# Two placements in a selective-scan kernel: where the old sum enters PSUM, and where a rounding term stands among the scans

## The chip, the cores and the metric

The kernel runs on one core of a Trainium2 chip. The metric is the device time of one execution in microseconds. Before the change it is 1489.29 us, the median of 3 runs (1488.71 to 1490.92).

## The reference, cut to what matters

Two layers of a state-space image model on a 64x64 image with 96 channels. Each layer normalises, projects to 192 inner channels, convolves 3x3, runs scans over the 4096 pixels in four orders, normalises, gates and projects back. The change touches only the scans of the second layer. Its core is this, with 192 channels and 16 states for each of the four orders:

```
delta = softplus(delta + delta_bias)
...
def step(h, t):
    u_t, d_t, B_t, C_t = t
    h = h * exp(d_t[..., None] * A[None]) + (d_t * u_t)[..., None] * B_t[:, :, None, :]
    y = einsum('bkdn,bkn->bkd', h, C_t)
    return (h, y)
...
y = out_y[:, 0] + out_y[:, 1, :, ::-1] + out_y[:, 2][:, :, i1] + out_y[:, 3][:, :, i2]
```

For each channel and state, h is a first-order recurrence along the pixels, with a decay exp(dt A) and an input dt u B. Then h is multiplied by C and summed over the 16 states, and the sums of the four orders are added.

## The kernel before, in words

**Tiling.** The second layer's scans are done in 16 groups (`GROUPS`, numbered 0 to 15): four orders, each in four chunks of 1024 pixels. In a group there are 24 units, numbered 0 to 23 here: 3 blocks of channels (T) times 8 pairs of states (m). A tile of a unit is 128x1024: 64 channels times two states on the partitions, 1024 pixels along. Units run in the order m = 0, 1 for T = 0, then T = 1, then T = 2 (units 0 to 5), then m = 2, 3, and so on. So T = 0, 1, 2 start with units 0, 2 and 4, and end with units 19, 21 and 23.

**What a unit does.** PSUM tile `b` first receives the factor B. For an even unit TensorE picks rows of B (`b<-B,selh`, `stage_B`), and VectorE multiplies by du in place, which is called the product here (`b<-b,du`, `stage_b`). For an odd unit ScalarE has already made products in another layout (`bT<-duT,BT`), and TensorE transposes them into PSUM (`b<-ident,bT`, `stage_t`), so VectorE has no product to make. Even units use PSUM tile b0, odd units b1, so each is refilled only after the scan two units before. ScalarE makes the decay (`a<-dt,am`, `stage_a`), VectorE runs the recurrence (`h<-a,b`, with `carry` when a chunk continues another, `stage_s`). GpSimd multiplies by C (`hc<-h,cb`, `stage_c`). TensorE sums over the partitions into the block's PSUM tile with a fold matrix (`ys<-hc,fold`, `stage_r`). After the last pair of states ScalarE copies that tile to y (`y<-ys`, `stage_y`).

**The old sum.** y already holds what earlier orders added. It enters the block's PSUM tile first, as a matmul of y with the identity (`ys<-y,ident`), and the folds of the 8 pairs are accumulated on top. Before the change this matmul stands in `stage_r` of the block's first unit, just ahead of that unit's fold. There is one PSUM tile for each T, so it can be filled only when `stage_y` of the group before has emptied it.

**C rows.** Each pair's C rows come from DRAM into one of 3 SBUF buffers (`cb<-C`, `fetch_c`), issued on SP's queue.

**Preparing the next group.** Beside the units of a group, the next groups' projections and step sizes are made (`prelude`). `pj<-u,xw` are the projections, in two halves, made a group further ahead (two groups before their use). `pd<-xd,dwb` is the argument of the softplus for one T. From it ScalarE makes |pd|, relu(pd), w = exp(-|pd|), ln = log(1 + w), and the rounded 1 + w written back to PSUM (`pd<-w,one`, step `plus`). VectorE then makes what that rounding added, (1 + w) - 1 - w (`w<-pd,w`, 128x512, step `missed`; the rounding term). GpSimd takes it off the logarithm (`ln<-ln,w`, step `found`), adds the relu (`sp<-sp,ln`, `whole`) and multiplies by u (`su<-sp,u`, `times`). The tiles w and ln exist once, so the next T's w waits for `found`, its ln for `whole`. Later SP's queue spreads sp and su to the dt and du tiles (`dt<-sp`, `du<-su`, four transfers each for each T).

**Order.** Every engine runs in program order here: the class `Ordered` wraps each call, and therefore nearly all these instructions carry its line, L859. The order is that of the main loop over j, the running number of units. A pass of the loop is called a slot here, numbered within its group like its unit. In slot j the loop issues, in this order: C transfers; `stage_B` or `stage_t` for unit j+1; a waiting `pd` matmul; the decay of unit j+2; the product, if j is even; `stage_r` of unit j-3 (LAG is 3); the scan of unit j; the carry of j-1; `stage_y` of unit j-4; `stage_c` of unit j-1; then the prelude steps due in that slot. `delta(T)` gives each of its steps a place in `slots`, plus 4T. In groups from 2 on `plus` and the logarithm stand in slots 1, 5 and 9, and `missed` in slots 2, 6 and 10, at the end of the slot, therefore behind that slot's scan. The `pd` matmul for T = 1 and 2 is issued in slots 3 and 7, the first half of `pj` in slot 11.

Of the kernel before, what the change touches and what calls it, by code (L numbers as in the profile page):

```python
# [44 lines left out]
def two_ss2d_layers(  # L45
# [678 lines left out]
    def scans(weights):  # L724

        xw, dwb, _ = weights
        with ExitStack() as sc:  # L730
            pre = sc.enter_context(tc.tile_pool(name="fpre", bufs=1))
            mn = sc.enter_context(tc.tile_pool(name="fmn", bufs=2))
            pps = sc.enter_context(tc.tile_pool(name="fps", bufs=1, space=PSUM))
            dram = sc.enter_context(tc.tile_pool(name="fdram", bufs=2, space=DRAM))
            carry = pre.tile([128, 3, NP], F32, name="fcarry")
            sums = pre.tile([128, 3], F32, name="fsums")
            xd = pre.tile([128, TC], F32, name="fxd")
            nc.vector.memset(xd[96:128], 1.0)
            halves = [slice(0, HT), slice(HT, TC)]
            load_exp_ln()  # L740

            def chunk(k, p, d, c):
                first = c == (NCH - 1 if d else 0)
                cols = TC // HW
                us = []
                for T in range(3):
                    ps = pps.tile([128, TC], F32, tag="m", name=f"fu{k}_{T}")
                    for h in range(2):
                        if p == 0:
                            nc.tensor.matmul(  # L750
                                ps[:, halves[h]], wide[h], u[T][:, HT * c : HT * (c + 1)],
                                start=True, stop=True,
                            )
                            continue
                        for q, s in enumerate(halves):
                            w0 = cols * c + cols // 2 * q
                            nc.tensor.matmul(
                                of_columns(ps[:, s], h), wide[h],
                                columns(u[T], h, slice(w0, w0 + cols // 2)), start=True, stop=True,
                            )  # L760
                    t = pre.tile([128, TC], F32, tag=f"us{T}", name=f"fus{k}_{T}")
                    nc.scalar.copy(t, ps)
                    us.append(t)
                ps = pps.tile([128, TC], F32, tag="m", name=f"fpj{k}")[0:NC]
                for s in halves:
                    for T in range(3):
                        nc.tensor.matmul(
                            ps[:, s], xw[0:64, 0, T, :], us[T][0:64, s],
                            start=(T == 0), stop=(T == 2),
                        )  # L770
                nc.scalar.copy(xd[0:NC], ps)
                C = dram.tile([NS, TC], F32, tag="C", name=f"fC{k}")
                nc.sync.dma_start(out=C, in_=xd[NC - NS : NC])
                B3 = pre.tile([NB, TC], BF16, tag="B3", name=f"fB3{k}")
                left = pre.tile([NB, TC], F32, tag="left", name=f"fleft{k}")
                nc.scalar.copy(B3, xd[0:NB])
                for r, of in ((32, xd), (64, xd), (64, left)):
                    q = slice(r, r + 32)
                    nc.gpsimd.tensor_sub(left[q], of[q], B3[q])
                    nc.gpsimd.tensor_copy(B3[q], left[q])  # L780

                for T in range(3):
                    ps = pps.tile([128, TC], F32, tag="m", name=f"fpd{k}_{T}")
                    for s in halves:
                        nc.tensor.matmul(
                            ps[:, s], dwb[96 : NC + 1, 0, T, :], xd[96 : NC + 1, s],
                            start=True, stop=True,
                        )
                    w, ln, t, dt, du, S = (
                        pre.tile([128, TC], F32, tag=nm, name=f"f{nm}{k}_{T}")  # L790
                        for nm in ("w", "ln", "t", "dt", "du", "S")
                    )
                    nc.scalar.activation(w, ps, AF.Abs)
                    nc.vector.tensor_scalar_max(dt, ps, 0.0)
                    nc.scalar.activation(w, w, AF.Exp, scale=-1.0)
                    nc.scalar.activation(t, w, AF.Identity, bias=one)
                    nc.scalar.activation(ln, w, AF.Ln, bias=one)
                    nc.vector.tensor_scalar_add(t, t, -1.0)
                    nc.vector.tensor_sub(w, w, t)
                    nc.vector.tensor_add(ln, ln, w)  # L800
                    nc.vector.tensor_add(dt, dt, ln)
                    nc.vector.tensor_mul(du, dt, us[T])
                    nc.vector.tensor_tensor_scan(
                        along(d, S), one.to_broadcast([128, TC]), along(d, dt),
                        0.0 if first else sums[:, T : T + 1], ALU.mult, ALU.add,
                    )
                    nc.scalar.copy(sums[:, T : T + 1], along(d, S)[:, TC - 1 : TC])
                    yp = pps.tile([128, TC], F32, tag="y", name=f"fy{k}_{T}")
                    for m in range(NP):
                        cb, a, b, wt, h = (  # L810
                            mn.tile([128, TC], F32, tag=nm, name=f"f{nm}{k}_{T}_{m}")
                            for nm in ("cb", "a", "b", "wt", "h")
                        )
                        row_of(C, m, cb)
                        B = pps.tile([128, TC], F32, tag="B", name=f"fB{k}_{T}_{m}")
                        for s in halves:
                            nc.tensor.matmul(B[:, s], pick(0, m), B3[:, s], start=True, stop=True)
                        nc.scalar.activation(a, dt, AF.Exp, scale=am[:, 0, 0, T, m : m + 1])
                        nc.scalar.activation(
                            wt, S, AF.Tanh, bias=lneps, scale=am[:, 1, 0, T, m : m + 1]  # L820
                        )
                        nc.vector.tensor_mul(b, B, du)
                        nc.vector.scalar_tensor_tensor(b, wt, 1.0, b, ALU.add, ALU.mult)
                        nc.vector.tensor_tensor_scan(
                            along(d, h), along(d, a), along(d, b),
                            0.0 if first else carry[:, T, m : m + 1], ALU.mult, ALU.add,
                        )
                        nc.scalar.copy(carry[:, T, m : m + 1], along(d, h)[:, TC - 1 : TC])
                        nc.gpsimd.tensor_mul(cb, h, cb)
                        for s in halves:  # L830
                            nc.tensor.matmul(
                                yp[:, s], fold2, cb[:, s], start=(m == 0), stop=(m == NP - 1)
                            )
                    for h, half in enumerate(HALF):
                        if p == 0:
                            to, of = y[T][half, HT * c : HT * (c + 1)], yp[half, halves[h]]
                        else:
                            to = columns(y[T][half], h, slice(cols * c, cols * (c + 1)))
                            of = of_columns(yp[half], h)
                        nc.vector.tensor_add(to, of, to)  # L840

            for k, (p, d, c) in enumerate(GROUPS):
                chunk(k, p, d, c)

    def scans(weights):

        xw, dwb, _ = weights  # L850
        class Ordered:
            def __init__(self, engine):
                self.engine = engine

            def __getattr__(self, name):
                op = getattr(self.engine, name)


                return lambda *args, **more: tc.keep_in_program_order(op(*args, **more))  # L859

        pe, act, dve, pool, sp = (
            Ordered(e) for e in (nc.tensor, nc.scalar, nc.vector, nc.gpsimd, nc.sync)
        )
        with ExitStack() as sc:
# [6 lines left out]
            LAG = 3  # L871
            halves = [slice(0, HT), slice(HT, TC)]
            state = [{} for _ in GROUPS]
            early = []

            xd = pre.tile([128, TC], F32, name="xd")
            dve.memset(xd[96:128], 1.0)
# [933 lines left out]
```

## Time and profile before

| what | value |
|---|---|
| median of 3 runs | 1489.29 us (1488.71 to 1490.92) |
| the profiled execution's own time | 1487.71 us |
| its span | 1485.9 us |
| second layer's groups, first scan of group 0 to last scan | about 285 to 1453 us |
| busy: VectorE (DVE), TensorE (PE), ScalarE (ACT), GpSimd (POOL) | 1354.1, 1233.7, 1209.1, 1100.7 us |
| scans of the groups (384) | 2.34 us with a carry, 2.28 us without |
| products (`b<-b,du`) | 1208 ns each |
| rounding terms (`w<-pd,w`) | 45, 665 ns each |
| old-sum matmuls (`ys<-y,ident`) | 120 records, median 592 ns |

The profile is of one execution. Its page gives busy time of each engine, waits and a chain of work; the timeline gives single instructions as start, length, engine, line, operation, output<-inputs and shapes, and in brackets the idle time before it with what ended it. A row can merge several instructions (x2, x6). A table by stretches gives, for each, its length, the busy time of PE, weight loads, DVE, ACT and POOL, TensorE's granted clock (1.00 is full) and the share and rate of the DMA engines. Ends of matmuls are modelled, and a matmul of fp32 data is recorded in several passes.

### The profile page before, as it was taken

How to read it: one execution, taken by the hardware profiler on the slowest of the kernel's cores; microseconds unless marked ns; L12 is line 12 of the kernel's file. 1: busy time of each engine (PE TensorE's matmuls, PEld its weight loads, DVE VectorE, ACT ScalarE, POOL GpSimd, SP SyncE). 2: the span in 40 equal slices, each digit the busy share in tenths (PEclk: the TensorE clock that was granted, in tenths of full speed). 3: DMA queues.
4: the chain of work that ended last, by engine and by line, in shares of the span. 5: the costliest groups of instructions: out<-in, count | busy, mean ns of one | idle time of the engine just before them, and what ended most of it. 6: DMA issues, size and time to landing. Idle time of an engine off the chain costs nothing.

```text
span 1485.9 us, 17265 instructions
## 1 busy us (share of the span) xinstructions
PE 1233.7 (83%) x5091; PEld 488.2 (33%) x5091; DVE 1354.1 (91%) x953; ACT 1209.1 (81%) x2492; POOL 1100.7 (74%) x595
## 2 busy tenths in 40 slices
PE   6954989688888888888887989888888888887887
PEld 3333333323232323333333333333333333322332
DVE  5957778679989999999999999999999999999998
ACT  6564355779889988998999999999998989897872
POOL 1003000479979999989898989898989898989891
PEclk9966988589899999999999999999999999999999
DMA  4230602516252626262626262626262626262534
GB/s 113 73 97 3 160 22 86 129 45 139 60 125 63 143 61 149 64 149 59 151 57 144 57 143 59 142 59 142 59 143 62 145 64 145 67 145 68 134 103 109
DMA packets 79793, 146.30 MB, mean 98 GB/s; under 512 B 27676, under 2 KB 30940, under 8 KB 79596
## 3 DMA queue, kind: packets, MB, share of 16 engines
q1 hardware_dynamic: 78540, 142.78, 39.2%
q0 software_dynamic: 576, 1.57, 0.4%
q8 instruction: 41, 0.67, 0.2%
q10 hardware_dynamic: 576, 0.79, 0.2%
q14 instruction: 60, 0.49, 0.1%
HBM read 80.85 MB, written 12.13 MB: 63 GB/s over the span
## 4 chain that ended last, share of the span: by engine, by line
DVE 30%; issue 21%; PE 14%; ACT 12%; POOL 6%; DMA 5%; SPq 3%; DVEq 0%; ACTq 0%; POOLq 0%
DVE h L859 19%; DVE b L859 8%; ACT a L859 4%; POOL hc L859 4%; PE ys L859 4%; PE pj L859 3%; ACT bT L859 3%; PE b L859 2%; SPq L859 2%; PE cp L1463 2%; DMA szt<-szd 1%; DMA xT<-xs 1%; PE in L1410 1%; PE pd L859 1%; POOL ln L859 1%
## 5 line engine op out<-in xcount | busy, mean ns | idle before, releaser
L859 POOL TENSOR_TENSOR hc<-h,cb 128x1024 f32<-128x1024 f32 x384 | 904.0, 2375 | 97.4 <-DVE h L859 47.1
L859 DVE TENSOR_TENSOR_SCAN h<-a,carry,b 128x1024 f32<-128x1024 f32 x288 | 664.9, 2337 | 27.9 <-PE b L859 5.9
L859 ACT ACTIVATE a<-dt,am 128x1024 f32<-128x1024 f32 x384 | 438.1, 1141 | 65.6 <-DVE h L859 60.5
L859 PE MATMUL ys<-hc,fold 128*64 128x512 f32 x1536 | 431.9, 642 | 1.3 <-POOL hc L859 1.2
L859 ACT ACTIVATE bT<-duT,BT 128x192 f32<-128x192 f32 x1012 | 387.4, 445 | 4.6 <-PE b L859 2.4
L859 PE MATMUL b<-ident,bT 128*128 128x128 f32 x1536 | 222.1, 289 | 25.3 <-DVE h L859 18.6
L859 DVE TENSOR_TENSOR b<-b,du 128x1024 f32<-128x1024 f32 x192 | 231.9, 1208 | 8.3 <-PE b L859 8.3
L859 DVE TENSOR_TENSOR_SCAN h<-a,b 128x1024 f32<-128x1024 f32 x96 | 216.3, 2278 | 12.4 <-POOL hc L859 3.0
L859 PEld LDWEIGHTS b<-ident,bT 128*128 128x128 f32 x1536 | 176.9, 147 | 149.2 <-DVE h L859 90.8
L859 PE MATMUL b<-B,selh 96*128 96x512 bf16 x384 | 117.5, 388 | 128.4 <-DVE h L859 128.0
L859 PEld LDWEIGHTS ys<-hc,fold 128*64 128x64 f32 x1536 | 78.2, 139 | 143.4 <-issue 104.2
L859 PEld LDWEIGHTS <-selh 96*128 96x128 bf16 x384 | 25.7, 98 | 257.6 <-DVE h L859 203.9
L859 PE MATMUL pj<-u,xw 64*124 64x512 f32 x192 | 101.1, 676 | 3.8 <-ACT sz L1445 2.0
L1488 DVE SCALAR_TENSOR_TENSOR acc<-pad,v,acc 128x1052 f32<-128x1052 f32 (+1 forms) x80 | 91.3, 1201 | 0.7
L859 POOL DMA_DIRECT2D du<-su x12 | 6.4, 536 | 82.9 <-ACT am L235 80.6
L261 POOL MEMSET nna<- 128x4 f32 (+1 forms) x9 | 1.0, 117 | 85.9 <-ACT nna L261 85.9
L859 PE MATMUL ys<-y,ident 128*128 128x512 f32 (+1 forms) x120 | 61.4, 616 | 0.0
L859 ACT CAST B<-pj 96x512 bf16<-96x512 f32 (+2 forms) x96 | 54.9, 575 | 6.3 <-PE pj L859 6.3
L859 POOL TENSOR_TENSOR sp<-sp,ln 128x512 f32<-128x512 f32 x45 | 57.9, 1286 | 0.2
L859 POOL TENSOR_TENSOR ln<-ln,w 128x512 f32<-128x512 f32 x45 | 58.0, 1288 | 0.0
L859 POOL TENSOR_TENSOR su<-sp,u 128x512 f32<-128x512 f32 x45 | 57.8, 1285 | 0.0
L859 PE MATMUL pd<-xd,dwb 29*64 29x512 f32 x192 | 57.6, 675 | 0.0
(185 smaller groups left out, 1195.1 us busy)
## 6 DMA issues: line engine op xcount, KB each, us to landing
cb<-C SPq DMA_DIRECT2D x256, 256.0 KB
dt<-sp SPq DMA_DIRECT2D x192, 128.0 KB
du<-su SPq DMA_DIRECT2D x180, 128.0 KB
szd<-sz SPq DMA_DIRECT2D x24, 256.0 KB
szt<-szd SPq DMA_DIRECT2D x24, 256.0 KB
xT<-xs SPq DMA_DIRECT2D x8, 384.0 KB
xs<-xT SPq DMA_DIRECT2D x1, 1536.0 KB
xs<-xT SPq DMA_DIRECT2D x8, 192.0 KB
```

What stands on the lines that cost most here:

```text
L261: return lambda *args, **more: tc.keep_in_program_order(op(*args, **more))
L859: return lambda *args, **more: tc.keep_in_program_order(op(*args, **more))
L1410: nc.tensor.matmul(ps[half], ipw_s[:, 64 * b : 64 * b + 64], xn[:, g * 512 : (g + 1) * 512], start=True, stop=True,)
L1463: nc.tensor.matmul(ps.rearrange("p (r w) -> p r w", w=HW), diag[:, k, :], pad[b][:, c, i : i + SR, j : j + HW], start=(k == 0), stop=(k == ...
L1488: nc.vector.scalar_tensor_tensor(acc, src, wk, acc, ALU.mult, ALU.add)
```

## The change

Three edits. First, a function `scans` is deleted that a later one of the same name replaces. Second, the old-sum matmul moves out of `stage_r` into a new function `start_sum`, which is put into the list of steps for the ends of slots 1, 2 and 4 (T = 0, 1, 2); it stood in slots 3, 5 and 7. The -1 puts it ahead of the other steps of its slot. Third, in groups from 2 on `missed` isn't issued where it stands but kept in a list `between`, and `plus` still stands in slot 1 + 4T; `missed` is now due at the end of that slot as well, and the loop issues it in the next slot behind the product and ahead of `stage_r` and the scan. For group 1 it is issued at once, where it was.

```diff
-    def scans(weights):
...
-            for k, (p, d, c) in enumerate(GROUPS):
-                chunk(k, p, d, c)
...
-            early = []
+            early, between = [], []
...
                     def missed():
 
-                        dve.scalar_tensor_tensor(
-                            me["w", T], me.pop(("pd", T)), -1.0, me["w", T], ALU.add, ALU.subtract
-                        )
+                        def step():
+                            dve.scalar_tensor_tensor(
+                                me["w", T], me.pop(("pd", T)), -1.0, me["w", T],
+                                ALU.add, ALU.subtract,
+                            )
+
+                        between.append(step) if k > 1 else step()
...
-                    o, slots = 4 * T, (-1, -1, -1, 0, 1, 1, 2, 3, 4, 5)
+                    o, slots = 4 * T, (-1, -1, -1, 0, 1, 1, 1, 3, 4, 5)
...
+            def start_sum(k, T):
+                p, d, c = GROUPS[k]
+                ps = live["y", T] = pps.tile([128, HT], F32, tag=f"y{T}", name=f"ys{k}_{T}")
+                parts = [(chunk(y[T], c), lambda s: s)] if (p, d) != (1, 0) else views(y[T], c)
+                for q, (view, f) in enumerate(parts):
+                    pe.matmul(f(ps), ident, view, start=(q == 0), stop=False)
+
             def stage_r(j):
...
-                if m == 0:
-                    ps = live["y", T] = pps.tile([128, HT], F32, tag=f"y{T}", name=f"ys{j}")
-
-                    parts = [(chunk(y[T], c), lambda s: s)] if (p, d) != (1, 0) else views(y[T], c)
-                    for q, (view, f) in enumerate(parts):
-                        pe.matmul(f(ps), ident, view, start=(q == 0), stop=False)
                 ps = live["y", T]
...
+            steps += [
+                (PER * k + (1, 2, 4)[T], -1, partial(start_sum, k, T))
+                for k in range(len(GROUPS)) for T in range(3)
+            ]
...
                 if j % 2 == 0:
                     unit(stage_b, j)
+                while between:
+                    between.pop(0)()
                 unit(stage_r, j - LAG)
                 unit(stage_s, j)
```

More of the change, by code (lines that the diff above doesn't have):

```diff
@@ L729, in scans @@
         xw, dwb, _ = weights
[L730 to L752, printed above, removed]
-                            )
[L754 to L840, printed above, removed]
-            for k, (p, d, c) in enumerate(GROUPS):
-                chunk(k, p, d, c)
@@ L845, in scans @@
-    def scans(weights):
-        xw, dwb, _ = weights
         class Ordered:
@@ L1024, in missed @@
                     def missed():
-                        dve.scalar_tensor_tensor(
-                            me["w", T], me.pop(("pd", T)), -1.0, me["w", T], ALU.add, ALU.subtract
-                        )
+                        def step():
[4 more added lines that the diff above has]
+                        between.append(step) if k > 1 else step()
                     def found():
```

## The prediction

> **What bounds the kernel now.** I read the head of the page, VectorE's waits in the sixteen groups (300 to 1460 us), and timelines of single groups. Below, "unit" is one of the 24 scans of a group, "slot" the loop pass of the same number.
>
> ```profile
> PE 1233.7 (83%) x5091; PEld 488.2 (33%) x5091; DVE 1354.1 (91%) x953; ACT 1209.1 (81%) x2492; POOL 1100.7 (74%) x595
> ```
>
> and the waits (total us, times, longest):
>
> ```profile
> DVE h L859 <- PE b L859: 7.1, 6, 2.5
> DVE b L859 <- PE b L859: 6.6, 6, 4.0
> DVE h L859 <- POOL hc L859: 3.0, 2, 2.6
> ```
>
> VectorE leads, and in the groups it waits for under 20 us in all. The timeline of group 4, units 10 and 11, on VectorE and then on ScalarE (start, length):
>
> ```profile
> 618.90 1.21 DVE L859 TENSOR_TENSOR b<-b,du 128x1024 f32<-128x1024 f32 x1
> 620.24 2.29 DVE L859 TENSOR_TENSOR_SCAN h<-a,b 128x1024 f32<-128x1024 f32 x1
> 622.44 0.67 DVE L859 SCALAR_TENSOR_TENSOR w<-pd,w 128x512 f32<-128x512 f32 x1
> 623.02 2.27 DVE L859 TENSOR_TENSOR_SCAN h<-a,b 128x1024 f32<-128x1024 f32 x1
> ```
>
> ```profile
> 619.65 0.72 ACT L859 ACTIVATE ln<-w,one 128x512 f32<-128x512 f32 x1 [0.75 <-POOL sp L859]
> 620.28 0.67 ACT L859 ACTIVATE pd<-w,one 128x512 f32<-128x512 f32 x1
> ```
>
> The scan starts 0.13 us after the product that it reads has ended; neighbours that don't read each other overlap by 0.08. So a group of VectorE alone is 12 x 5.84 (product, two scans, their joints) + 3 x 0.58 (rounding terms less overlap) = 71.8 us. Measured from scan 0 to scan 0, groups 5 to 14 take 72.24 on average.
>
> A second loop is as long. GpSimd of group 5 and SP's queue behind it:
>
> ```profile
> 669.34 4.68 POOL L859 TENSOR_TENSOR hc<-h,cb 128x1024 f32<-128x1024 f32 x2 [2.95 <-DMA cb<-C]
> ...
> 708.23 11.67 POOL L859 TENSOR_TENSOR hc<-h,cb 128x1024 f32<-128x1024 f32 x5
> ...
> 741.59 4.67 POOL L859 TENSOR_TENSOR hc<-h,cb 128x1024 f32<-128x1024 f32 x2 [1.47 <-DMA cb<-C]
> ```
>
> ```profile
> 717.62 1.08 SPq L859 DMA_DIRECT2D cb<-C  x2
> ...
> 736.08 2.46 SPq L859 DMA_DIRECT2D cb<-C  x4
> ```
>
> From hc of unit 1 to the end of hc of unit 16 (717.60) GpSimd is never idle: 48.3 us, the same within 0.12 in eight groups. That end frees a cb buffer; SP then issues 30 transfers in a row (19 to 20 us), the last being cb of pair 1, which lands about 4 us later and lets the next group's hc 1 begin. hc 1 starts follow each other by 72.18 us on average (669.34 to 1391.18, ten groups), about 72.0 without the pieces in which GpSimd waited for VectorE.
>
> TensorE is third. Its clock is granted in steps:
>
> ```profile
> 400.87:404.28 3.41, 1.91 (x9) 0.55 (x8) 3.41 (x3) 2.55 (x7) 3.41 (x3) 1.00 0.00 0
> 404.28:407.69 3.41, 3.41 (x5) 1.31 (x5) 3.28 (x3) 1.70 (x4) 3.41 (x3) 0.50 0.21 72
> 694.41:697.82 3.41, 1.91 (x9) 0.40 (x7) 3.41 (x3) 2.94 (x9) 3.41 (x3) 1.00 0.00 0
> 1349.77:1353.18 3.41, 1.69 (x8) 0.31 (x6) 3.41 (x2) 1.91 (x5) 3.41 (x2) 1.00 0.54 151
> 1353.18:1356.60 3.42, 3.07 (x12) 1.86 (x12) 3.29 (x3) 2.61 (x7) 3.42 (x3) 0.50 0.56 150
> ```
>
> (stretch and length, TensorE busy first; granted clock third from the end.) A stretch with 1.69 us of busy TensorE is followed by half clock; 1.91 went either way. In group 1 half clock fell on slot 11:
>
> ```profile
> 402.50 0.60 PE L859 MATMUL b<-B,selh 96*128 96x512 bf16 x2 [1.50 <-DVE h L859]
> ...
> 404.04 5.28 PE L859 MATMUL pj<-u,xw 64*124 64x512 f32 x6
> ```
>
> ```profile
> 411.33 2.35 DVE L859 TENSOR_TENSOR_SCAN h<-a,carry,b 128x1024 f32<-128x1024 f32 x1 [2.45 <-PE b L859]
> ```
>
> Group 5 has the same six matmuls at 697.73 in 2.84 us. VectorE lost 2.54 + 1.02 + 0.68 = 4.2 us in group 1 from there.
>
> **What the Trainium skill says.** "TensorE: Matmul & The Clock Gate", section The HAM clock gate: the clock is half or full, decided from activity in free-running windows of about 3.4 us. The trace agrees, in steps of 3.41, but here a window more than half busy was enough to lose it. "Perfetto Trace Analysis", section DVE / Act Engine Instruction: an engine's own semaphore is raised only once the write is acknowledged, which is later than the next instruction may begin. The trace shows this as +0.13 against -0.08. No page prices the rounding term's place; its rows do.
>
> **The change, part by part.**
>
> Deleting the first `scans`: a name defined twice; no instruction changes.
>
> Rounding term, groups 2 to 15 (42 of 45; made one group ahead). Before: product, +0.13, scan, -0.08, term, -0.08, scan. After: product, term, scan, scan, all with -0.08, since the scan waits for the product's count, which is up while the term runs. -0.03 becomes -0.24: 0.21 us each, 8.8 us in all. That the overlap holds behind a product is not shown; nothing to 0.21 bounds it, and I take 0.21. New wait: the term needs ScalarE's pd<-w one scan earlier, and scan and GpSimd's hc stand behind it. Set side by side for all 42 in the timelines, that result ends before the product of the same slot in 33 cases and after it in 9, by 0.02 to 0.85 (above: 620.95 against 620.11). Those delays sum to 4.9 us with 0.15 for signal and lost overlap. ScalarE was itself waiting for GpSimd's sp there, so this wait holds VectorE to GpSimd's pace.
>
> Old y: per group 3 matmuls of 128x512 (6 records, or 12 of half size), about 1.05 us each at full clock, leave slots 3, 5, 7 for the ends of slots 1, 2, 4. Their count is unchanged, and no transfer moves. They now wait for ScalarE's copy that empties the same bank; it ends about 1.8 us after a scan that TensorE has already passed, so I cost it at nothing. What it relieves: unit 5. Its transposes end 0.14 us before its scan in ten of the fourteen groups 1 to 14 (every other odd unit has 0.7 us or more nearly always), and the sum of scan 5's delays is 6.7 us, among them 1.81, 1.82 and 1.64 where half clock stretched the old-y pair to 2.08. Without it ahead, 1.0 to 2.1 us less work precedes these transposes: 6.7 us gone.
>
> Group 0 pays: two old-y products, 1.9 us each at half clock, now stand ahead of the second pj (5.48 us) and of b for unit 4, where VectorE already waits 3.99. I take 1.7 us, between -1 (clock back earlier) and +3.5.
>
> VectorE alone would thus need 71.8 - 0.63 = 71.2 a group; GpSimd and SP hold 72.0 to 72.1. About 1 us per group is then slack, and of the gains 4 to 5 us survive: 2.4 in group 1 (VectorE-bound), the rest from removed waits of GpSimd.
>
> The idle time also moves. At slot 10 TensorE waits for scan 10: product + 0.13 + scan before, product + term + scan after. Its 1.50 us becomes 1.50 + 0.58 - 0.21 = 1.87, more where the term waits for ScalarE. Windows that hold it all had 1.91 busy; they will have 1.54, under the 1.69 that lost the clock. Slot 11 follows with b, the fold and six pj matmuls. Before, transposes 13 had 0.77 us to spare; with the term no longer behind scan 10, 0.19. Half clock adds 1.7 us per window. So I expect group 1's loss, 4.2 us, wherever a window lies over this gap. The gap of 1.87 must lie inside by some 1.6 us: (3.41 + 1.87 - 3.2) / 3.41, about 60% at a random phase; a group lengthened by a loss shifts phase. I take 5 of 13 groups (1 to 13; the last have no pj). Each costs 4.2 - 1.0 slack = 3.2.
>
> Sum: 5 x 3.2 = 16.0; 8 others x -0.14 (72.24 to 72.1) = -1.1; group 1's wait and terms -2.4; its present loss half likely to go, -2.1; group 0 +1.7. Total +12.1. The profiled execution took 1487.7 us (span 1485.9), so 1499.8; it lies 1.6 under the median of 1489.3, so about 1501.
>
> **Rivals.**
>
> GpSimd's loop is the bound and slot 10 keeps its clock: -2.4 - 2.1 - 2.0 (half of the removed waits) + 1.7, about -5: 1484, between 1480 and 1488. For it: 1.91 us mostly kept the clock, and old y elsewhere raises activity. Against: the gap does grow. This ends on the other side; it decides if fewer than two groups lose slot 11.
>
> VectorE keeps all: -8.8 - 6.7 + 1.7 = -14, 1475. Against it, hc 1 waits for its transfer in every group.
>
> The term's waits eat its gain: 4.9 us grow to some 9, because VectorE arrives earlier at an unchanged ScalarE result, against 8.8 gained: 1487 to 1491. For it, the nine late rows are nearly all at the third term. Against, GpSimd's stretches absorb it.
>
> **How the numbers follow.** Slot 11 losing its clock 0.52 (1493 to 1515, with two to nine groups); GpSimd's loop 0.26; the term's waits 0.12; VectorE keeping all 0.10. The range 1477 to 1515 leaves out the lower half of the last and the worst of the first. 0.2% is 3 us, about what a measurement here can tell from none. Faster: 0.10 + three quarters of 0.26 + little = 0.32; same 0.15; slower 0.53.
>
> **What would show it.** Product to term and term to scan at -0.08, no 0.13 there; scan 5 no longer behind TensorE; TensorE's wait in slot 10 at 1.9 us or more; pj at 5 us in several groups and scan 13 waiting there. I am wrong if pj stays at 2.8 us throughout: then hc 1 to hc 1 near 72 us speaks for GpSimd's loop, and near 71.2 for VectorE.

## The result, and the profile after

The changed kernel takes 1551.74 us (median of four runs, 1549.51 to 1557.21); the kernel before, beside it, 1489.00 (1484.39 to 1490.92). The ratio is 1.0441 with an interval of 1.0414 to 1.0467. The forecast was 1501 with 1515 as its upper end: the direction and the mechanism were right, the size was off by a factor of five.

The deleted function moves the lines: what was L859 is now L738. The head of the page of the changed kernel, and its row of the projections `pj`:

```profile
PE 1283.9 (83%) x5091; PEld 506.5 (33%) x5091; DVE 1352.0 (87%) x953; ACT 1209.2 (78%) x2492; POOL 1101.5 (71%) x595
...
L738 PE MATMUL pj<-u,xw 64*124 64x512 f32 x192 | 127.2, 821 | 3.7 <-ACT sz L1335 2.0
```

No engine has more instructions. VectorE is even 2.1 us less busy, TensorE 50 us more, at the same number of matmuls: its clock, granted at 0.893 of full on average against 0.929. A `pj` matmul takes 821 ns on average, 676 before. VectorE's waits between 300 and 1520 us of the changed kernel (total us, times, longest):

```profile
DVE h L738 <- PE b L738: 53.5, 13, 4.7
DVE b L738 <- PE b L738: 20.0, 26, 1.8
DVE w L738 <- ACT pd L738: 11.6, 16, 1.5
```

Before, the first of these rows was 7.1 us, the second 6.6, and the third did not exist. Where it happens is seen in one group. The timeline of group 9, slots 10 to 16, on VectorE:

```profile
1020.71 1.21 DVE L738 TENSOR_TENSOR b<-b,du 128x1024 f32<-128x1024 f32 x1
1023.02 0.69 DVE L738 SCALAR_TENSOR_TENSOR w<-pd,w 128x512 f32<-128x512 f32 x1 [1.09 <-ACT pd L738]
...
1036.37 2.35 DVE L738 TENSOR_TENSOR_SCAN h<-a,carry,b 128x1024 f32<-128x1024 f32 x1 [4.57 <-PE b L738]
1039.65 1.23 DVE L738 TENSOR_TENSOR b<-b,du 128x1024 f32<-128x1024 f32 x1 [0.94 <-PE b L738]
...
1046.20 1.23 DVE L738 TENSOR_TENSOR b<-b,du 128x1024 f32<-128x1024 f32 x1 [0.59 <-PE b L738]
```

and on TensorE:

```profile
1026.02 1.04 PE L738 MATMUL b<-B,selh 96*128 96x512 bf16 x2 [3.06 <-DVE h L738]
1026.98 1.98 PE L738 MATMUL ys<-hc,fold 128*64 128x512 f32 x4
1028.89 5.48 PE L738 MATMUL pj<-u,xw 64*124 64x512 f32 x6
1034.30 1.97 PE L738 MATMUL b<-ident,bT 128*128 128x128 f32 x8
```

The third rounding term waits 1.09 us for ScalarE. Scan 10 stands behind it, so TensorE has nothing to do for 3.06 us, loses its clock, and runs b, the fold, `pj` and the transposes of unit 13 at half speed. Scan 13 waits 4.57 us for them, the products of slots 14 and 16 a further 0.94 and 0.59. The table by stretches (stretch, length, busy time of PE, weight loads, DVE, ACT and POOL, granted clock, share and rate of the DMA engines) shows the window that lost the clock and one that follows it:

```profile
1022.09:1025.50 3.41, 0.87 (x4) 0.00 (x0) 2.48 (x2) 3.37 (x8) 3.41 (x3) 1.00 0.00 0
...
1028.92:1032.33 3.41, 3.41 (x6) 1.42 (x5) 2.75 (x2) 0.54 (x2) 3.41 (x3) 0.50 0.51 144
```

The same happens in 12 of the 13 groups 1 to 13, all but group 11 (there TensorE was still working off an earlier half clock, and its gap was 0.91 us), and each time for 10.2 to 13.7 us (three or four windows). Before, it was one group. From scan 0 of group 1 to scan 0 of group 15 the changed kernel takes 1078.15 us, before 1016.09: these 62.06 us make up the difference of the spans (1547.6 against 1485.9). Group 9 can be added up: 72.10 before, less three terms at 0.21 and a wait of 0.17 at scan 5 that is gone, plus 1.18, 4.65, 1.02 and 0.68 for the four waits above (idle time, plus the overlap or the shorter joint that a wait takes away), gives 78.83; from scan 0 at 992.12 to scan 0 at 1070.93 are 78.81.

### The profile page after: what moved, and what is told of

Same layout as the page of the kernel before. It is cut to its first block, busy times and chain, and to the rows that moved or that the text cites. A ratio compares the mean times of both kernels' runs of the same rounds, so it can differ in the third digit from the quotient of the medians.

```text
span 1547.6 us, 17299 instructions
## 1 busy us (share of the span) xinstructions
PE 1283.9 (83%) x5091; PEld 506.5 (33%) x5091; DVE 1352.0 (87%) x953; ACT 1209.2 (78%) x2492; POOL 1101.5 (71%) x595
## 3 DMA queue, kind: packets, MB, share of 16 engines
q0 software_dynamic: 576, 1.57, 0.4%
## 5 line engine op out<-in xcount | busy, mean ns | idle before, releaser
L738 POOL TENSOR_TENSOR hc<-h,cb 128x1024 f32<-128x1024 f32 x384 | 903.6, 2367 | 156.3 <-DVE h L738 100.3
L738 DVE TENSOR_TENSOR_SCAN h<-a,carry,b 128x1024 f32<-128x1024 f32 x288 | 660.8, 2334 | 55.6 <-PE b L738 40.8
L738 ACT ACTIVATE a<-dt,am 128x1024 f32<-128x1024 f32 x384 | 438.2, 1141 | 54.3 <-DVE h L738 48.3
L738 PE MATMUL ys<-hc,fold 128*64 128x512 f32 x1536 | 444.9, 660 | 1.6 <-POOL hc L738 1.6
L738 ACT ACTIVATE bT<-duT,BT 128x192 f32<-128x192 f32 x1012 | 386.5, 445 | 2.0
L738 PE MATMUL b<-ident,bT 128*128 128x128 f32 x1536 | 236.5, 298 | 29.3 <-DVE h L738 19.6
L738 DVE TENSOR_TENSOR b<-b,du 128x1024 f32<-128x1024 f32 x192 | 232.5, 1211 | 22.0 <-PE b L738 22.0
L738 PEld LDWEIGHTS b<-ident,bT 128*128 128x128 f32 x1536 | 188.5, 152 | 151.9 <-DVE h L738 96.5
L738 PE MATMUL b<-B,selh 96*128 96x512 bf16 x384 | 124.3, 407 | 136.1 <-DVE h L738 134.5
L738 DVE TENSOR_TENSOR_SCAN h<-a,b 128x1024 f32<-128x1024 f32 x96 | 215.0, 2274 | 20.4 <-PE b L738 12.7
L738 PE MATMUL pj<-u,xw 64*124 64x512 f32 x192 | 127.2, 821 | 3.7 <-ACT sz L1335 2.0
L738 PEld LDWEIGHTS ys<-hc,fold 128*64 128x64 f32 x1536 | 79.8, 142 | 145.1 <-issue 107.2
L738 PEld LDWEIGHTS <-selh 96*128 96x128 bf16 x384 | 27.2, 101 | 262.5 <-DVE h L738 219.7
L738 ACT COPY xd<-pj 124x512 f32<-124x512 f32 x32 | 18.7, 585 | 79.2 <-PE pj L738 79.2
L738 ACT CAST B<-pj 96x512 bf16<-96x512 f32 (+2 forms) x96 | 55.0, 576 | 21.0 <-PE pj L738 21.0
L738 PEld LDWEIGHTS pj<-u,xw 64*124 64x124 f32 x192 | 43.0, 243 | 85.1 <-issue 62.4
L738 POOL DMA_DIRECT2D du<-su x12 | 6.4, 538 | 83.0 <-ACT am L235 80.8
L738 POOL TENSOR_TENSOR ln<-ln,w 128x512 f32<-128x512 f32 x45 | 57.6, 1280 | 0.0
L738 POOL TENSOR_TENSOR sp<-sp,ln 128x512 f32<-128x512 f32 x45 | 57.3, 1274 | 0.2
L738 POOL TENSOR_TENSOR su<-sp,u 128x512 f32<-128x512 f32 x45 | 57.2, 1272 | 0.0
```

## The experiments

Theory A is that of the prediction: the term ahead of scan 10 widens TensorE's gap in slot 10, the clock halves over `pj`, and scan 13 waits. Its rivals: B, the moved old sum is the cause; C, the term's own wait for ScalarE; and a fourth, that any change of phase locks the group to whole windows.

**One half of the change each.** The first run calls `start_sum` in `stage_r` again, where the old-sum matmuls stood; the second takes the rounding term back.

```diff
 # the term alone moved
 def stage_r(j):
+    if m == 0:
+        start_sum(k, T)
...
-steps += [(PER * k + (1, 2, 4)[T], -1, partial(start_sum, k, T)) ...]
```

> Only the rounding term is moved; the old y stays in slots 3, 5 and 7. Theory A (the term ahead of scan 10 widens TensorE's gap in slot 10, the clock halves over pj in slot 11): the loss stays, about 6.3 us in 10 to 13 groups, so 1540 to 1565 us, with pj near 5.3 us there and scan 13 waiting 4 us or more. Theory B (the old y, gone from slots 3, 5 and 7, is what costs the clock): no loss here, 1480 to 1490. Theory C (the term's wait for ScalarE costs): its 11.6 us appear, about 1495 to 1500.

```diff
 # the old sum alone moved
-between.append(step) if k > 1 else step()
+step()
...
-o, slots = 4 * T, (-1, -1, -1, 0, 1, 1, 1, 3, 4, 5)
+o, slots = 4 * T, (-1, -1, -1, 0, 1, 1, 2, 3, 4, 5)
```

> Only the old y is moved; the rounding term stays behind the scan. Theory A: the gap in slot 10 stays 1.50 us, at most two groups lose the clock over pj, scan 5 no longer waits: 1480 to 1489 us. Theory B: the loss of the changed kernel is here, 1535 to 1560. Theory C: like A. A fourth, that any shift of phase makes the kernel fall into a repeating loss (period 78.5 us, 23 windows of 3.413): 1520 to 1560 although nothing was widened.

The term alone: 1543.1 us, ratio 1.0336 (1.0285 to 1.0387), with half clock over slot 11 in ten of the groups 1 to 13 (counted in its profiled execution, the longest of its four: 1555.0 us, the others 1531.8 to 1543.1). The old sum alone: 1488.7, ratio 0.9994 (0.998 to 1.0008), no such group. B is out. In the run with the term alone, group 2 shows a loss without any lateness of the term. On TensorE and on VectorE:

```profile
483.85 0.61 PE L738 MATMUL b<-B,selh 96*128 96x512 bf16 x2 [1.87 <-DVE h L738]
484.38 1.31 PE L738 MATMUL ys<-hc,fold 128*64 128x512 f32 x4
485.62 5.48 PE L738 MATMUL pj<-u,xw 64*124 64x512 f32 x6
```

```profile
480.85 0.68 DVE L738 SCALAR_TENSOR_TENSOR w<-pd,w 128x512 f32<-128x512 f32 x1
...
493.10 2.35 DVE L738 TENSOR_TENSOR_SCAN h<-a,carry,b 128x1024 f32<-128x1024 f32 x1 [3.47 <-PE b L738]
```

The gap is 1.87 us, to the digit what the prediction worked out, the term has waited for nobody, and the clock is lost all the same: C in its plain form is out too. The fourth rival is out with the old sum alone: a moved phase, and no repeated loss.

The old sum alone also shows why its gain of 6.7 us does not arrive. Its undisturbed groups take 71.90 us in place of 72.09, but TensorE now loses its clock around slot 6, in groups 5, 10 and 13, which take 74.60, 73.83 and 73.96. The old sum was work that stood in slots 3 to 7; that its absence there is the cause is likely, but no run tests it alone. The waits of unit 5 are gone, and others have come: in group 5, 2.09 us at scan 9.

**Work in the gap that does nothing.** The changed kernel, with one matmul of a zero 128x128 matrix and 512 columns of y, added to the sum of T = 0 in slot 10, behind that slot's fold; it adds zero.

```diff
+if j < N and j % PER == 10:
+    pe.matmul(live["y", 0], zero, chunk(y[0], ...), start=False, stop=False)
```

> The changed kernel with one more matmul in slot 10 of every group: a zero 128x128 matrix times 512 columns of y, added into the sum of T = 0 (adds zero). It fills about 1.0 us of the gap. Theory A: the clock stays full over pj, no wait at scan 13, 1478 to 1487 us, group period about 72. Theory C: the term's waits remain, 1490 or more. If what matters is the load and not the gap, it is no faster than the changed kernel, 1550.

1500.6 us, ratio 1.0081 (1.0052 to 1.011): four groups lose slot 11 in place of twelve, though TensorE has more to do. The waits of scans fall from 53.5 to 22.7 us. That is more than the 1478 to 1487 expected of A, because one matmul does not close the gap: in the four groups 1.70 to 2.46 us of it were left, and the terms still waited 10.9 us for ScalarE. But more load with a smaller gap was faster by 51 us: the cause is the idle time of TensorE, not its load.

**The third term alone back.**

```diff
-between.append(step) if k > 1 else step()
+between.append(step) if k > 1 and T < 2 else step()
...
+if T == 2 and k > 1:
+    slots = (-1, -1, -1, 0, 1, 1, 2, 3, 4, 5)
```

> The changed kernel, with the third rounding term of a group (T = 2, slot 10) back behind its scan; T = 0 and 1 stay ahead of theirs. Theory A: the gap in slot 10 is 1.50 us again, no loss over pj in most groups: 1479 to 1488 us. Theory B: the loss stays, 1535 to 1560. Theory C: only the waits of T = 2 go, about 1540.

1489.9 us, ratio 0.9996 (0.998 to 1.0013), just above the expected 1488, and one group with half clock over slot 11. Of 42 terms, the 14 in slot 10 make the whole loss. The other 28 gain nothing in sum: groups without a loss run at 71.4 us, but half clock at slots 5 and 6 comes in six groups and gives it back. The first two terms widen the gaps there; with the old sum alone moved it was three groups, so both edits may have a part in it.

**Real work in the gap.** The first half of `pj` is issued at the end of slot 10 in place of slot 11.

```diff
-}.get(k, ((-13, -12, -11, -10), (-10, -9, -8, -7), -9, -6.8, -5.95))
+}.get(k, ((-14, -12, -11, -10), (-10, -9, -8, -7), -9, -6.8, -5.95))
```

> The changed kernel with the first half of pj (three matmuls of 64x512, 2.84 us at full clock) issued one slot earlier, at the end of slot 10 in place of slot 11, so that TensorE has real work in the gap behind scan 10. Nothing is added. Theory A (the gap in slot 10 costs the clock, and pj in slot 11 is where the loss hurts): slot 11 loses its clock in at most three groups in place of twelve, scan 13's waits shrink from 54 us to under 15, and about 60 us come back: 1478 to 1492. If the loss belongs to slot 11 whatever stands in slot 10, or pj itself is too light to hold the clock, the half clock stays and so does the time, over 1530.

The second run also puts the `pd` matmuls of T = 1 and 2 at the ends of slots 2 and 6.

```diff
+if k > 1 and T:
+    steps.append((begin[0] - 1, begin[1]))
+else:
     early.append((PER * (k - 1) + begin[0], begin[1]))
```

> As the run with pj in slot 10, and the pd matmuls of T = 1 and 2 issued at the ends of slots 2 and 6 in place of the starts of slots 3 and 7, so that the gaps behind scans 2 and 6 are filled as well. Theory A: losses at slots 3 and 6, which the runs with fewer terms moved showed, become rarer; 0 to 6 us under the run with pj alone, 1474 to 1486, and faster than the kernel before. If these gaps cost nothing that VectorE waits for, it equals the run with pj alone within 3 us; if pd so placed comes too late for ScalarE's softplus, the terms wait and it is slower by 5 us or more.

1489.1 us, ratio 0.9988 (0.9976 to 1.0), and 1489.0, ratio 1.0006 (0.9985 to 1.0027). In neither does a group from 1 to 13 run all of `pj` at half clock, and none has a wait at scan 13; the 62.7 us are back by moving three matmuls one slot. In two groups of the second a window of half clock starts at the end of `pj`. Group 9 of the first, on TensorE:

```profile
982.69 1.08 PE L738 MATMUL ys<-hc,fold 128*64 128x512 f32 x4
983.70 2.84 PE L738 MATMUL pj<-u,xw 64*124 64x512 f32 x6
986.47 0.60 PE L738 MATMUL b<-B,selh 96*128 96x512 bf16 x2
```

There is no idle bracket in front of b, and `pj` takes 2.84. But neither is faster than the kernel before, which the second was expected to be. VectorE's waits of the first show where the gain went:

```profile
DVE w L738 <- ACT pd L738: 12.4, 16, 1.6
DVE h L738 <- PE b L738: 8.3, 7, 1.6
```

The terms wait 12.4 us for ScalarE, against the 8.8 that moving them saves, and of the 8.3 us of scan waits 6.2 are at scan 9, in five groups with half clock around slot 6. With the clock of slot 11 held, the time lies where the prediction's third rival put it (the term's waits eat its gain, 1487 to 1491), but that rival had only the first of these two in its sum. The second run fills the gaps of slots 2 and 6 as well and gains nothing: its terms wait 11.7 us, and half clock around slot 6 stays in four groups. The `pd` matmuls use 29 rows of the array's 128.

**The gap alone.** The kernel before, with VectorE operations between product and scan in slot 10 that compute nothing used.

```diff
 if j % 2 == 0:
     unit(stage_b, j)
+if j < N and j % PER == 10:
+    for _ in range(2):
+        dve.scalar_tensor_tensor(idle, idle, -1.0, idle, ALU.add, ALU.subtract)
```

> The kernel before, with two idle VectorE operations on a zero tile of 128x256 between product and scan in slot 10 of each group. They read nothing of PSUM, wait for nobody and leave every value as it is; the old sum, the rounding terms and their waits stay as before. TensorE's gap in slot 10 grows from 1.50 to about 2.1 us. Direct cost 16 x 0.6 = 10 us. Theory A (the width of the gap alone takes the clock): half clock over pj in slot 11 in six or more of groups 1 to 13 and scan 13 waits there by 2 to 4 us, 1520 to 1550. Theory C (the term's own wait for ScalarE does the harm) and theory B (the old sum): no half clock in slot 11, direct cost alone, 1496 to 1503.

1612.7 us, ratio 1.086 (1.0815 to 1.0904), beyond both expectations: the operations did not take the 0.3 us assumed. Their row (ns, shortest, median and longest):

```profile
L859 DVE SCALAR_TENSOR_TENSOR idle<-idle x32: 415/1394/4541, 325.4 to 1533.0; 128x256 f32<-128x256 f32 x32
```

So the gap was 2.96 to 6.18 us, and all of the groups 1 to 13 lost slot 11. This says nothing of a small gap; it shows that a wide gap takes the clock with every term, every old sum and every wait on ScalarE where it was before. A second run copies 128x384 of the finished product out of PSUM, which took 558 ns each time:

```diff
+if j < N and j % PER == 10:
+    dve.tensor_scalar_add(idle, live["b", j][:, 0 : 3 * HT // 4], 0.0)
```

> The kernel before, with one VectorE copy of 128x384 out of PSUM (the product just made, into a spare tile) between product and scan in slot 10 of each group; values stay as they are. In the run with two SBUF operations there they took 0.4 to 4.5 us each in place of the 0.3 assumed, so the gap grew to between 2.96 and 6.2 us and said nothing of small widths. Reading PSUM like the rounding term, this one should take about 0.5, and TensorE's gap in slot 10 should be 1.50 + 0.42 = 1.9 us, nearly the 1.87 that moving the term makes without any lateness. Direct cost 16 x 0.42 = 7 us. If a gap of 1.9 takes the clock by chance of phase, as the prediction had it (about 60%), some 6 to 10 groups of 1 to 13 lose slot 11 at about 4 us each: 1515 to 1545. If only the wider gaps of 2.4 to 3.4 us, which the late term makes, do it: at most three groups, 1495 to 1508.

1527.5 us, ratio 1.0256 (1.021 to 1.0302). The gap is 1.87 us (1.80 to 1.81 in three groups), and seven of the groups 1 to 13 lost slot 11: 54%, where the prediction had put 60% for this width. Which groups, the phase decides, that is, where the gap lies in the windows. On TensorE, group 3, which lost its clock, and group 6, which kept it:

```profile
553.77 0.60 PE L859 MATMUL b<-B,selh 96*128 96x512 bf16 x2 [1.87 <-DVE h L859]
554.31 1.09 PE L859 MATMUL ys<-hc,fold 128*64 128x512 f32 x4
555.33 5.48 PE L859 MATMUL pj<-u,xw 64*124 64x512 f32 x6
```

```profile
784.88 0.60 PE L859 MATMUL b<-B,selh 96*128 96x512 bf16 x2 [1.87 <-DVE h L859]
785.41 1.08 PE L859 MATMUL ys<-hc,fold 128*64 128x512 f32 x4
786.42 2.83 PE L859 MATMUL pj<-u,xw 64*124 64x512 f32 x6
```

and the windows over the two gaps:

```profile
551.83:555.24 3.41, 1.54 (x8) 0.31 (x6) 3.41 (x3) 2.00 (x5) 3.41 (x3) 1.00 0.00 0
780.53:783.94 3.41, 2.10 (x12) 1.05 (x12) 3.38 (x4) 3.38 (x8) 3.41 (x3) 1.00 0.00 0
783.94:787.35 3.41, 2.47 (x8) 0.78 (x9) 3.41 (x3) 3.21 (x8) 3.41 (x2) 1.00 0.00 0
```

In group 3 the whole gap lies in one window, which then has 1.54 us of work, the prediction's number. In group 6 a border of windows at 783.94 cuts the same gap in two, and both parts stay above 2 us. This is theory A with nothing else in it.

**The lateness of the third term.** The changed kernel, with ScalarE's `plus` one slot earlier, straight behind w.

```diff
-o, slots = 4 * T, (-1, -1, -1, 0, 1, 1, 1, 3, 4, 5)
+o, slots = 4 * T, (-1, -1, -1, 0, 1, 0, 1, 3, 4, 5)
```

> The changed kernel with ScalarE's rounded 1 + w (step plus) one slot earlier, straight behind w in slots 0, 4 and 8 in place of slots 1, 5 and 9, so that the rounding term no longer waits for it. The term's waits for ScalarE, 11.6 us in the changed kernel, should fall under 2, and TensorE's gap in slot 10 to 1.87 us in every group, from 2.4 to 3.4. If a gap of 1.87 is enough by chance of phase: 6 to 10 groups of 1 to 13 lose the clock in slot 11, at about 5 us each, 1515 to 1540. If the lateness is what loses it (theory C in a new form): at most three groups, 1478 to 1495. If the loop of the group locks to whole windows whatever the gap: 11 or more groups, 1540 and more.

1522.6 us, ratio 1.0233 (1.0183 to 1.0283), seven groups. It fell short of its purpose, as its waits show:

```profile
DVE h L738 <- PE b L738: 29.5, 9, 4.7
...
DVE w L738 <- ACT ln L738: 8.2, 11, 1.5
```

The term writes w in place, and ScalarE's logarithm still reads w. So the term now waits for `ln` in place of `pd`, in five groups of 1 to 13 for over half a microsecond. Of those five groups (gaps 2.78 to 3.50) four lost the clock; of the other eight (1.59 to 2.13) three did.

All runs but the one with the zero matmul, put together by the width of the gap (TensorE's longest idle stretch around scan 10, groups 1 to 13, read off the timelines):

| gap in slot 10, us | groups | half clock over slot 11 |
|---|---|---|
| under 1.43 | 58 | 4 |
| 1.43 to 1.52 | 47 | 2 |
| 1.59 | 1 | 0 |
| 1.80 to 1.95 | 23 | 13 |
| 2.10 to 2.13 | 3 | 1 |
| 2.41 and over | 37 | 35 |

(The four in the first row are in kernels with `pj` in the gap: one or two windows that begin at or within `pj`, and at most 0.22 us of wait at scan 13.)

The prediction held that a gap costs the clock when some 1.6 us of it lie in one window. With the borders of the windows taken from the moments at which the granted clock changes, the 64 gaps of 1.59 us and more sort almost cleanly by the longest part that lies in one window:

| longest part of the gap in one window, us | groups | half clock over slot 11 |
|---|---|---|
| up to 1.63 | 13 | 0 |
| 1.64 to 1.77 | 7 | 5 |
| 1.84 and over | 44 | 44 |

The two gaps over 2.41 us that kept the clock (2.78 and 2.81) had 1.57 and 1.53 in their fuller window. So width and place account for the losses, with the term late or not, and no lock of the loop to the windows is needed.

**The other loop.** The prediction held that GpSimd, the `cb` buffer and SP's queue would keep a group at 72.0 to 72.1 us, and took 1.0 us per group off for it. Two kernels test that, the one with `pj` and `pd` in the gaps and the kernel before, each with the C rows of pair 1 of the next group fetched one slot earlier on SP's queue (`fetch_c`):

```diff
-for ahead, odd in ((4, 0), (1, 1)):
+for ahead, odd in ((4, 0), (1, 1), (2, 1)):
...
-    if i % 6 == 0 and 0 <= k < len(GROUPS):
+    if i % 6 == 0 and 0 <= k < len(GROUPS) and (
+        odd == 0 or (ahead == 2) == (i == 0 and k > 0)
+    ):
```

> As the run with pj and pd in the gaps, with the C rows of pair 1 of the next group fetched one slot earlier on SP's queue, ahead of the last spread of sp and su. If the loop of GpSimd, cb buffer and SP's 30 issues holds the group at 72.0 us, as the prediction had it, the period falls towards VectorE's own 71.2 and the time by 5 to 12 us against the run without. If VectorE's own work and its waits for TensorE set the period, the time is the same within 3 us.

> The kernel before with nothing but the C rows of pair 1 of the next group one slot earlier on SP's queue. If the loop of GpSimd, cb buffer and SP held the kernel before at 72.0 to 72.2 us a group while VectorE needed 71.8, this gains 14 x 0.3 = 4 us, 1483 to 1488, and hc of unit 1 starts within 0.4 us of its scan. If VectorE alone set the period, the same time within 2 us.

With `pj` and `pd` in the gaps: 1481.4 us, ratio 0.9958 (0.9943 to 0.9973). The kernel before with this edit alone: 1482.9, ratio 0.9953 (0.993 to 0.9977). Both are faster than the kernel before, by about 7 us, and the expectations had put such times down to GpSimd's loop. The groups say otherwise. Scan 0 of groups 6 and 7 of the kernel before, then of the kernel with the C rows ahead:

```profile
735.27 4.58 DVE L859 TENSOR_TENSOR_SCAN h<-a,carry,b 128x1024 f32<-128x1024 f32 x2
...
807.36 4.58 DVE L859 TENSOR_TENSOR_SCAN h<-a,carry,b 128x1024 f32<-128x1024 f32 x2
```

```profile
730.16 4.58 DVE L859 TENSOR_TENSOR_SCAN h<-a,carry,b 128x1024 f32<-128x1024 f32 x2
...
802.25 4.58 DVE L859 TENSOR_TENSOR_SCAN h<-a,carry,b 128x1024 f32<-128x1024 f32 x2
```

Both are 72.09 us apart, though the wait of hc 1 for `cb<-C` (1.47 us in this group before) is gone and hc 1 starts within 0.43 us of the end of its scan in every group. Groups 6 to 10 have the same length in the two kernels within 0.02 us. So VectorE takes 72.09 there by itself, not 71.8, and the loop behind GpSimd had not set it: in group 6 of the second kernel its instructions with their joints come to 71.9, and a delay of 0.16 at scan 5 is the rest. In the profiles, groups 1 to 14 are 8.7 us shorter, most of it in group 1 (78.04 us before, 71.90 now: no half clock over slot 11) and group 5 (73.73 against 72.08: no wait at unit 5, 1.82 us before); the spans differ by 6.2, because group 1 starts 3.2 us later. Whether the C rows keep these two from losing the clock, or only moved the phase, these runs don't settle.

With `plus` early as well:

> As the run with C rows ahead (pj and pd in the gaps, C rows of pair 1 earlier), with the rounded 1 + w one slot earlier as well. Its 8.0 us of term waits should go; VectorE is then alone as the bound: 1473 to 1481, 0 to 8 us under the run with C rows ahead. If ScalarE, with the step earlier, delays the decays or the odd units' products, it is the same or slower.

1481.2 us, ratio 0.9924 (0.9899 to 0.9949), no better than 1481.4 without it. Three of its groups with a carry (1, 3 and 11) take 71.2 us, what the prediction gave VectorE alone. In groups 6 to 9 a term waits for `ln` by 0.9 to 1.4 us, in others a product waits for TensorE.

## Why the prediction was wrong, by its steps

**The bound and the mechanism: right.** VectorE sets the groups, the wider gap in slot 10 takes TensorE's clock, `pj` at half clock makes scan 13 wait. The gap of 1.87 and the window with 1.54 us of work came out to the digit where the term was not late, and the 1.6 us that must lie in one window held as well. The chance of about 60% fits 13 of 23 gaps of 1.80 to 1.95 us, though these are not independent draws, since the place of a gap follows from the group before.

**The step that failed first: "I take 5 of 13 groups".** It was 12. The prediction set ScalarE's result and the product of before side by side, found nine of 42 late by up to 0.85 us, and let those rows stand for after. But with the first two terms moved VectorE is 0.42 us earlier at product 10. In slot 10 ScalarE's `pd` came on average 0.01 us before the product's end in the kernel before (14 groups, from 0.99 earlier to 0.85 later); in the changed kernel it comes 0.67 after it, late in all 14 groups, by 0.34 to 1.42 (of this shift of 0.68 the 0.42 explains the larger part; the rest is not traced). In group 9 the product of slot 10 ends at 1021.92, and ScalarE's row ends at 1022.91:

```profile
1022.24 0.67 ACT L738 ACTIVATE pd<-w,one 128x512 f32<-128x512 f32 x1
```

The gap is then not 1.87 but 2.41 to 3.43 us in the 12 groups that lost the clock, and at that width 35 of 37 groups lost it. "More where the term waits for ScalarE" stood in the text, and was not carried into the count. The halving from 60% of 13, 8 groups, to 5 had no row behind it either: it rested on "a group lengthened by a loss shifts phase". The prediction's own formula, (3.41 + gap - 3.2) / 3.41, gives 77 to 100% for the twelve measured gaps, 10.4 groups in sum, and twelve were lost. Three of the gaps (groups 8, 9 and 10), by their windows, which keep 0.77 to 1.16 us of work:

```profile
943.59:947.00 3.41, 0.77 (x4) 0.00 (x0) 2.16 (x2) 3.41 (x8) 3.41 (x3) 1.00 0.00 0
1022.09:1025.50 3.41, 0.87 (x4) 0.00 (x0) 2.48 (x2) 3.37 (x8) 3.41 (x3) 1.00 0.00 0
1100.60:1104.01 3.41, 1.16 (x6) 0.20 (x4) 2.97 (x3) 3.02 (x7) 3.41 (x3) 1.00 0.00 0
```

Nine of the twelve groups took 78.0 to 78.8 us, close to 23 windows of 3.4133 (78.51), so the gap moves by 0.15 of a window at most from such a group to the next. It is tempting to call this a lock, but before, with 72.09 us or 21.1 windows, the gap moved as little. That a loss keeps the next gap in place, or shifts it out, as the prediction had it, is not shown.

**The price, "4.2 - 1.0 slack = 3.2": mis-sized.** Measured: the twelve groups average 77.88 us, those of before without group 1 72.16, so 5.72 net of all gains. The 4.2 was group 1's, with 0.77 us to spare at the transposes and part of the chain still at full clock. The prediction had the 0.19 that remains and did not use it. All four matmul rows at half clock (1.04, 1.98, 5.48, 1.97) are 4.86 us longer than at full (0.60, 1.08, 2.84, 1.09); less 0.19 that is 4.67, and scan 13 waits 4.57 plus the lost overlap of 0.08. The late term adds about 0.9 and the products 14 and 16 about 1.5. The slack of 1.0 us did not exist: groups 11 and 14 of the changed kernel, without a loss, took 71.77 and 71.79, and groups of later runs with no late term 71.2, under the 72.0 at which GpSimd's loop was to hold them.

Together: 12 x 5.72 = 68.7, less 0.8 for groups 11 and 14 and 5.9 for the loss that group 1 already had, gives the 62.1 us measured from group 1 to 15. The prediction's sum has 5 x 3.2 = 16.0 in place of the 68.7; with twelve groups at its price it would have been 38.4, so count and price both failed.

**Rounding term, 0.21 each: right where nothing waits.** Product to term stands at -0.09 and term to scan at -0.08 in the 27 of 42 places without a wait; the bound from nothing to 0.21 fell at its upper end. Its waits were put at 4.9 us and were 11.6.

**Old y, 6.7 us gone: half right.** The waits at unit 5 are gone in every run with the old sum moved. Alone, the edit is worth nothing measurable, with half clock around slot 6 in three groups in their place. **Group 0, +1.7:** 82.92 before, 80.58 after, a gain of 2.3 in these two executions, outside the bounds of -1 and +3.5. One pair decides little: in the nine profiles with the old sum moved group 0 takes 79.1 to 82.8, in the three with the old sum in place and slot 10 untouched or its term moved 81.9 to 82.9.

**The rivals.** That GpSimd's loop is the bound fell. The term's waits eating its gain gave the right time once the clock of slot 11 was held, but half clock around slot 6 had a share in it. VectorE keeping everything is seen only in single groups at 71.2.

## What to carry to other kernels

An idle stretch moved onto an engine whose clock depends on its activity has a price that depends on its width and on what runs next: before an instruction is put ahead of another engine's trigger, work out that engine's gap, see how much of it can fall into one window of the clock's, and see whether the heaviest work that nobody hides comes right behind it. If it does, put that work into the gap; here three matmuls one slot earlier were worth 62 us. And a wait that is added must be measured against where its engine will arrive after the change, all edits together, not against the rows of before.

## What the runs showed of the hardware

- **Half clock needs no idle window.** The Trainium skill, "TensorE: Matmul & The Clock Gate", section HAM oscillation — how this bites in real kernels, gives as the abstract rule that TensorE should have no idle gaps over about 3.4 us. Here a gap of 1.87 us was enough in 13 of 23 cases at 1.80 to 1.95, and a window with 1.54 us of work of 3.41 lost the clock: the measurement decides.
- **Work on few rows holds the clock less.** The prediction saw windows with 1.91 us of busy TensorE go either way. The lost one at 400.87 (group 1, with a gap of 1.50) has 0.24 us of `pj` in it, which uses 64 rows of 128 (the first number of its shape), the kept one at 694.41 has 0.09. If each stretch of busy time is multiplied by the rows of its matmul over 128, they come to 1.67 and 1.75. Over the profiles of all 14 kernels (3730 windows at full clock, from 300 us to the start of group 14), half clock followed 218 of 221 windows with under 1.50 us counted so, 47 of 98 with 1.50 to 1.70, and 14 of 3411 with more. By plain busy time, 187 of the 1412 windows with 1.8 to 2.8 us were followed by half clock, with no clear border. It fits that the `pd` matmuls, on 29 rows, did not hold the clock at slot 6. No run changed the rows alone, so that they are the cause is argued, not shown.
- **A loss lasts whole windows.** In the changed kernel half clock over slot 11 lasted 10.2 to 13.7 us, three or four windows of 3.41, and so it did with the wide gap alone.
- **A VectorE operation with two SBUF inputs lasted until GpSimd's instruction beside it had ended.** In the run with the wide gap the same 128x256 operation took 0.42 us when GpSimd was idle and up to 4.54 when it was not, ending about 0.3 us after the end of GpSimd's instruction. The copy out of PSUM in the next run took 0.558 us (0.557 to 0.559) 16 times, with GpSimd busy beside it each time. "GPSIMD Engine Reference", section 1. Specifications, names this contention of GpSimd with VectorE instructions that have two SBUF inputs; the trace agrees.
